# Attention woven into a feed-forward kernel: fewer tile visits, a re-timed plan, and sums moved to GpSimd

## The chip, the cores and the metric

The kernel runs on one core of a Trainium2 chip. A core has five engines that run side by side, each through its own instructions in order: TensorE (PE in the profile; its weight loads are PEld), VectorE (DVE), ScalarE (ACT), GpSimd (POOL), and SyncE (SP), which here issues the DMAs. They wait for each other by semaphores. The metric is the device time of one execution, in microseconds; lower is better.

## The reference

A macaron block on `x` of 8 x 512 x 512 numbers in float32: half a feed-forward block, attention, and half a feed-forward block again, each behind a layernorm.

```python
x = x + 0.5 * ffn(layernorm(x));  x = x + attn(layernorm(x));  x = x + 0.5 * ffn(layernorm(x))

# ffn: 512 -> 2048 -> 512
h = silu(x @ w_gate) * (x @ w_up)
h = keep, in each group of four neighbours, the two of largest magnitude
return h @ w_down

# attn: 16 query heads of 32, 4 key/value heads (tiled over the query heads), rotary positions
scores = einsum('bhqd,bhkd->bhqk', Qr, Kr) / HEAD_DIM ** 0.5
out = einsum('bhqk,bhkd->bhqd', softmax(scores), V_rep)
return out.reshape(b, s, d) @ W_o
```

## The kernel before

There are 8 batches and two feed-forward blocks for each, so 16 blocks (`blocks`). Attention of one batch runs beside the feed-forward products of another, and so does the layernorm of the next block. All instructions are written in one order by a Python program that plans as it goes: `at` holds a clock for TensorE, VectorE and ScalarE, `takes` books a step on one of them with a time written in the code, and `later`/`soon` put VectorE work into queues that `fill` empties when it fits beside TensorE's clock. `ensure` runs the queued work that a step depends on at once. Nothing is moved afterwards: each engine gets its instructions in the order in which the program names them.

*Feed-forward.* Gate and up are computed by a scheme with seven products of half-size blocks (`woven`, L604) in place of eight; their sums of weight quarters (S1 to S4) are made once, in the first block, by VectorE (`combine_gu`, L673), and stored to DRAM. One such product is four matmuls of 128 x 128 by 256 in the program, eight in the trace, as each float32 matmul runs as two. The down product does the same (`products`, L532), with five sums of down-weight quarters (`SUMS`) for each half of the hidden size, also made in the first block: `combine_down` loads 1 MB (`raw`), VectorE adds (L482), SP stores (L483). After each chunk of 512 hidden numbers, `keep_two_of_four` makes the selection on VectorE (L392 to L418) in two halves, and GpSimd makes the sums of `h` that the down products take (L424 to L429).

*Attention.* For each batch: layernorm, projections with rotary positions, then four groups `c` of four query heads. TensorE works these in tiles of 32 rows (`sc`, the scores, L817; `st`, the transposed scores, L850 and L855) or 32 columns (`ops`, the weighted values, L865; `den`, the denominators, L883), four heads side by side. For each of four blocks of keys `t`, ScalarE makes `p = exp(st)` (L858) and VectorE adds up the `p` of the blocks in place (`summed`, L157 in the profile since queued work is run from one line); `den` then takes the sum of the last one, and `divided` (L880 on) divides by a logarithm and an exponential. Scores of group `c + 1` are computed ahead, VectorE finds their maxima (`nm`), `in_pieces` splits these into three bfloat16 parts (`z`), and `pieces_by_row` transposes them (`tr`), for a subtraction inside the next `st`. `sc` and `st` share one PSUM buffer, `p` has two buffers, and all other products share three PSUM banks (`Bank`), taken in rotation.

*The visits.* `attention` is a generator. At each `yield` it hands back a function that tells when it may go on; the main loop at the end runs feed-forward products, counts them in `n` (0.5 for a product of `woven`, 1 for a down product), and goes on with a side stage when `n` is past its `due` and its inputs are ready by the plan. So a visit is a stretch of attention's matmuls between feed-forward products. Before the change, each block `t` of keys has two visits, one with `weighted(t - 1)` and `scores(c + 1, t)`, one with `exponentials(c, t)`, and each group has one more, with `weighted(NT - 1)` alone. `WEIGHTS` gives the share of time for each visit.

Of the kernel before, what the change touches and what calls it, by code (L numbers as in the profile page):

```python
# [18 lines left out]
P = 128  # L19
# [7 lines left out]
def macaron_block(  # L27
# [123 lines left out]
    class Later:  # L151
# [8 lines left out]
        def fits(self, slack):  # L160
            return max(at["dve"], self.ready) + self.us <= at["pe"] + slack

# [76 lines left out]
    def transposed(parts):  # L239
# [5 lines left out]
        takes("pe", 0.65 if kind == FP else 0.45)  # L245
# [5 lines left out]
    def now():  # L251
        return 0.0

    in_xT = []

    def layernorm_t(got, tag, src=None, xb=None):
# [54 lines left out]
        if xb is None:  # L311
# [11 lines left out]
            yield now  # L323
            for t in range(NT):
                normalise(t)
                end = at["act"]
                yield now if t < NT - 1 else lambda: end if len(in_xT) < 2 else None
            for t in range(NT):
                turn(t)
                yield now  # L330
# [40 lines left out]
    def keep_two_of_four(h, made, sums=None, halves=(0, 1)):  # L371
# [14 lines left out]
        for half in halves:  # L386
# [32 lines left out]
            if sums is not None:  # L419
# [5 lines left out]
                else:  # L425
# [3 lines left out]
                    nc.gpsimd.tensor_tensor(h21, h21, h11, ALU.subtract)  # L429
            thin["halves"] = half + 1  # L430
# [15 lines left out]

    gu_made, written = {}, {}
# [21 lines left out]
    def combine_down():  # L469

        for c in range(NCH):
# [8 lines left out]
            def combine(i, name, c=c, quarter=quarter, sums=sums):  # L480
                op = ALU.add if name[2] == "+" else ALU.subtract
                nc.vector.tensor_tensor(sums[:, i], quarter[name[:2]], quarter[name[3:]], op)  # L482
# [20 lines left out]
    def ffn(b, final, last):  # L503
# [9 lines left out]
        def products(hs, g):  # L513

            operands = []

# [4 lines left out]
            def product(i):  # L521
# [17 lines left out]
                takes("pe", 3.69)  # L539
# [17 lines left out]
        def down(h, w, c, t):  # L557
# [7 lines left out]
            takes("pe", 3.62)  # L565
# [6 lines left out]
        def hidden(h, i, r, cols):  # L572

            n = cols.stop - cols.start
            for m in range(2):
# [6 lines left out]
                takes("pe", 3.62 * n / S)  # L582
# [10 lines left out]
        def woven(h, i, r, last_one):  # L593
# [5 lines left out]
            def product(bank, q, rhs, first, ready=0.0):  # L599
# [12 lines left out]
                takes("pe", 1.83)  # L612
# [139 lines left out]
    def attention(b):  # L752
# [15 lines left out]
        def projected(dst, col, scale):  # L768
# [6 lines left out]
            takes("pe", 3.62)  # L775
# [28 lines left out]
        takes("pe", 3.75)  # L804
# [8 lines left out]
        def scores(c, t, nm):  # L813
# [6 lines left out]
            takes("pe", 1.15)  # L820
# [24 lines left out]
        def exponentials(c, t, mT):  # L845
# [10 lines left out]
            takes("pe", 1.45)  # L856
# [5 lines left out]
        def weighted(t, ops, p):  # L862
# [5 lines left out]
            takes("pe", 1.1)  # L868

        def summed(p, before):  # L870
# [219 lines left out]
```

## Time and profile before

| what | value |
|---|---|
| time, median of 3 runs | 3265.1 us (3264.68 to 3265.1) |
| profiled execution: time, span | 3262.97 us, 3261.2 us |
| granted TensorE clock over the span | 0.997 |
| busy in the first 125 us: TensorE, VectorE, GpSimd | 101.21, 85.32, 15.66 us |
| busy from 125 us on: TensorE, VectorE, GpSimd | 3098.76, 2176.40, 548.61 us |
| sums of exponentials on VectorE | 384, 248.4 us, 700 ns each |
| down sums on VectorE | 20, 14.3 us, 757 ns each |
| ScalarE's table loads | 216, 277.1 us |

The span runs from the first to the last instruction of the core. Busy time of TensorE is drawn from modelled ends and overlapping rows; the start times of its matmuls are the firmer reading. In a row of the waits, the engine, line and tile that waited stand first, then whom it waited for, then the total in us, how often, and the longest. In the timeline, the first number is the start in us, the second the duration; brackets at the end hold the idle time just before and who ended it.

### The profile page before, as it was taken

The page shows a single profiled execution, that of the slowest core. Times are in us where ns is not written, and L with a number is a line of the kernel's source. Part 1 is how long each engine was busy: PE and PEld are TensorE (multiplying, and loading weights), DVE is VectorE, ACT ScalarE, POOL GpSimd, SP SyncE. Part 2 cuts the span into 40 slices and gives each one's busy share as a digit, 9 for nine tenths or more (in the row PEclk, how much of TensorE's full clock was granted, in tenths as well). Part 3 has the DMA queues.
Part 4 walks back from the last instruction along what each step waited for, and adds up shares of the span by engine and source line. Part 5 has one row for each costly group of instructions (what it writes and reads, how often), then busy time and mean ns, then how long its engine had stood idle before and what let it go on. Part 6 is the DMA issues. An engine that isn't in the chain of part 4 may idle for free.

```text
span 3261.2 us, 43693 instructions
## 1 busy us (share of the span) xinstructions
PE 3200.0 (98%) x15880; PEld 2316.7 (71%) x15880; DVE 2261.7 (69%) x4892; ACT 1196.7 (37%) x1686; POOL 564.3 (17%) x868
## 2 busy tenths in 40 slices
PE   7999999999999999999999999999999999999999
PEld 5786667766667677766776668766766678666886
DVE  6767775778577775776578865777577765777554
ACT  2222552155324451354314442155325542255221
POOL 0221112210130112110221111211120121201120
PEclk9999999999999999999999999999999999999999
DMA  7563334543433444334453345433533436234451
GB/s 244 196 221 108 116 127 145 174 130 101 158 134 126 136 139 162 133 118 138 143 172 129 110 154 176 140 119 117 196 97 115 155 126 210 91 117 135 156 174 46
DMA packets 249285, 463.21 MB, mean 142 GB/s; under 512 B 24432, under 2 KB 64368, under 8 KB 248304
## 3 DMA queue, kind: packets, MB, share of 16 engines
q1 hardware_dynamic: 249072, 460.42, 42.9%
q8 instruction: 127, 2.08, 0.3%
q14 instruction: 86, 0.70, 0.1%
HBM read 421.53 MB, written 38.80 MB: 141 GB/s over the span
## 4 chain that ended last, share of the span: by engine, by line
PE 92%; DVE 4%; DMA 2%; ACT 1%; issue 0%; POOL 0%; SPq 0%; DVEq 0%; ACTq 0%
PE x L604 25%; PE y L532 23%; PE v L604 12%; PE z L604 6%; PE proj L772 4%; PE sc L817 4%; PE st L850 4%; PE ops L865 4%; PE y L944 3%; PE tr L244 1%; PE gu L579 1%; DMA xn<-x 1%; DVE nm L157 1%; PE den L883 1%; PE vps L797 1%; PE y L562 1%
## 5 line engine op out<-in xcount | busy, mean ns | idle before, releaser
L604 PE MATMUL x<-ts,w 128*128 128x256 f32 x3000 | 721.5, 383 | 10.7 <-DVE corner L618 9.2
L604 PEld LDWEIGHTS x<-ts,w 128*128 128x128 f32 x3000 | 560.0, 190 | 165.5 <-issue 50.1
L532 PE MATMUL y<-wd,h 128*128 128x256 f32 x1984 | 457.3, 385 | 12.0 <-DVE h L418 6.3
L532 PEld LDWEIGHTS y<-wd,h 128*128 128x128 f32 x1984 | 375.8, 192 | 101.3 <-issue 32.0
L858 ACT ACTIVATE p<-st 128x2048 f32<-128x2048 f32 x128 | 239.6, 1872 | 400.7 <-PE st L855 233.2
L424 POOL TENSOR_TENSOR e<-h 128x512 f32<-128x512 f32 x62 | 89.3, 1440 | 1615.4 <-DVE h L418 1442.7
L157 DVE TENSOR_REDUCE nm<-sc 128x1 f32<-128x512 f32 x512 | 320.2, 681 | 68.8 <-PE sc L817 66.9
L532 PE MATMUL y<-wd,e 128*128 128x256 f32 x1488 | 337.3, 381 | 0.2 <-PE den L883 0.2
L545 DVE SCALAR_TENSOR_TENSOR x<-y,x 128x512 f32<-128x512 f32 x372 | 241.9, 683 | 130.2 <-PE y L532 128.6
L532 PEld LDWEIGHTS y<-wd,e 128*128 128x128 f32 x1488 | 279.7, 190 | 62.3 <-issue 18.7
L236 ACT ACT_TABLE_LOAD x216 | 277.1, 1283 | 4.5 <-PEq L1079 0.7
L224 ACT COPY row<-x 128x512 f32<-128x512 f32 x212 | 124.1, 585 | 392.5 <-PE x L604 392.1
L157 DVE TENSOR_TENSOR p<-p 128x512 f32<-128x512 f32 x384 | 248.4, 700 | 10.4 <-PE ops L865 10.4
L653 ACT ACTIVATE h<-x 128x256 f32<-128x256 f32 x125 | 47.5, 380 | 558.1 <-PE x L604 525.0
L604 PE MATMUL v<-xT,w 128*128 128x256 f32 x1000 | 241.5, 385 | 5.7 <-DVE corner L226 5.7
L604 PE MATMUL v<-ts,w 128*128 128x256 f32 x1000 | 240.1, 383 | 1.1 <-DVE h L157 1.1
L604 PE MATMUL x<-xT,w 128*128 128x256 f32 x1000 | 240.5, 383 | 0.0
L604 PE MATMUL z<-xT,w 128*128 128x256 f32 x1000 | 240.0, 383 | 0.0
L604 PEld LDWEIGHTS v<-xT,w 128*128 128x128 f32 x1000 | 187.3, 191 | 57.3 <-issue 13.2
L604 PEld LDWEIGHTS x<-xT,w 128*128 128x128 f32 x1000 | 185.3, 190 | 57.4 <-issue 30.6
L604 PEld LDWEIGHTS v<-ts,w 128*128 128x128 f32 x1000 | 186.8, 190 | 54.8 <-issue 20.8
L604 PEld LDWEIGHTS z<-xT,w 128*128 128x128 f32 x1000 | 185.8, 190 | 52.6 <-issue 22.9
(106 smaller groups left out, 4010.4 us busy)
## 6 DMA issues: line engine op xcount, KB each, us to landing
w<-gu SPq DMA_DIRECT2D x472, 256.0 KB, 3.3
w<-in_w_gu SPq DMA_DIRECT2D x394, 256.0 KB, 3.3
wd<-wd SPq DMA_DIRECT2D x155, 512.0 KB, 3.8
wd<-in_w_down SPq DMA_DIRECT2D x124, 256.0 KB, 5.0
x<-x SPq DMA_DIRECT2D x64, 256.0 KB, 2.6
xn<-x SPq DMA_DIRECT2D x64, 256.0 KB, 7.0
x<-in_x SPq DMA_DIRECT2D x32, 256.0 KB, 3.4
gu<-w SPq DMA_DIRECT2D x32, 256.0 KB, 2.6
```

The source lines that it names most:

```text
L157: self.does()
L224: nc.scalar.copy(dst, src)
L236: nc.scalar.activation(dummy[:, 1:2], dummy[:, 0:1], f)
L532: nc.tensor.matmul(out=y.tile[:, t, :], lhsT=part[:, t * P : (t + 1) * P], rhs=operands[i][:, n, :], start=(n == 0), stop=(n == 3),)
L545: nc.vector.scalar_tensor_tensor(to, y.tile, 0.5 * sign, to, ALU.mult, ALU.add)
L604: nc.tensor.matmul(out=bank.tile[:, m, :], lhsT=lhs[:, m, k, :], rhs=rhs[:, k, :], start=(first and m == 0 and k == 0), stop=(k == 1), ski ...
L772: nc.tensor.matmul(out=ps.tile, lhsT=wa[:, k, col : col + P], rhs=xT[:, k, :], start=(k == 0), stop=(k == ND - 1))
L817: nc.tensor.matmul(out=sc[:, kv, :], lhsT=qT[rows, c, t * P : (t + 1) * P], rhs=kT[rows, :], start=True, stop=True)
L850: nc.tensor.matmul(out=st[:, kv, :], lhsT=kT[rows, t * P : (t + 1) * P], rhs=qT[rows, c, :], start=True, stop=False)
L858: nc.scalar.activation(p, st, AF.Exp)
L865: nc.tensor.matmul(out=ops[rows, :], lhsT=v[:, t, rows], rhs=p[:, kv, :], start=(t == 0), stop=(t == NT - 1))
L944: nc.tensor.matmul(out=y.tile, lhsT=qT[:, k, t * P : (t + 1) * P], rhs=wo[:, k, :D], start=(k == 0), stop=(k == ND - 1))
```

## The change

Five things change together.

- **The plan's times.** `multiplied` books TensorE's steps with new, shorter times and adds `SWITCH` where the shape changes between whole and tiled matmuls. `Bank` takes the bank that comes free first instead of the next in rotation. A fourth clock stands for GpSimd.
- **Visits.** `weighted(NT - 1)` moves into the next group's first visit, `divided` and `in_pieces` move behind `exponentials` into its visit, and in the last group, where there are no scores, the two visits of a block of keys become one.
- **Sums of exponentials.** Of the four heads, GpSimd sums two and VectorE two.
- **Down sums.** GpSimd makes all of them, issued at once and not queued, in two stages at other places (from `n` = 11 and from 22, not from 9 to 25).
- **Layernorm.** Normalising and transposing wait until ScalarE's booked time is at most `BEHIND` = 2 us ahead of TensorE's (`by_scalar`).

```diff
-    HEARD, TOLD = 0.2, 0.15
-    at = {"pe": 0.0, "dve": 0.0, "act": 0.0}
+    HEARD, TOLD, SWITCH, BEHIND = 0.2, 0.15, 0.1, 2.0
+    at = {"pe": 0.0, "dve": 0.0, "act": 0.0, "pool": 0.0}
...
+    tiled = [False]
+
+    def multiplied(us, tiles=False):
+
+        takes("pe", us + (SWITCH if tiles != tiled[0] else 0.0))
+        tiled[0] = tiles
...
+    class Done:
+
+
+        def __init__(self, end):
+            self.end = end
...
     class Bank:
         def __init__(self, shape, name, dtype=FP):
-            self.slot = banks.popleft()
+            self.slot = min(banks, key=lambda slot: max(slot[2], when(slot[1]), at["pe"]))
+            banks.remove(self.slot)
...
+    def by_scalar():
+
+        return at["act"] - BEHIND
...
-            yield now
+            yield by_scalar
             for t in range(NT):
                 normalise(t)
                 end = at["act"]
-                yield now if t < NT - 1 else lambda: end if len(in_xT) < 2 else None
+                yield by_scalar if t < NT - 1 else lambda: max(end, by_scalar()) if len(in_xT) < 2 else None
...
-    def combine_down():
-
-        for c in range(NCH):
+    def combine_down(g):
+
+        for c in range(2 * g, 2 * g + 2):
             raw = p_slots.tile([P, 4, D], FP, "raw")
             nc.sync.dma_start(out=raw, in_=w_down[c])
...
-            def combine(i, name, c=c, quarter=quarter, sums=sums):
+            for i, name in enumerate(SUMS):
                 op = ALU.add if name[2] == "+" else ALU.subtract
-                nc.vector.tensor_tensor(sums[:, i], quarter[name[:2]], quarter[name[3:]], op)
-                nc.sync.dma_start(out=combined[c // 2, name][:, c % 2 * 2 : c % 2 * 2 + 2, :], in_=sums[:, i])
-
-            for i, name in enumerate(SUMS):
-                made = later(0.7, partial(combine, i, name), at["pe"], for_later)
-            p_slots.used(wa_slots.used(made))
+                nc.gpsimd.tensor_tensor(sums[:, i], quarter[name[:2]], quarter[name[3:]], op)
+                nc.sync.dma_start(out=combined[g, name][:, c % 2 * 2 : c % 2 * 2 + 2, :], in_=sums[:, i])
             yield now
-        ensure([made])
+        done_down.add(g)
...
-                takes("pe", 1.83)
+                multiplied(1.73)
...
-            takes("pe", 1.15)
+            multiplied(1.07, True)
...
         def summed(p, before):
 
             if before is None:
                 return []
-            for kv in range(N_KV):
-                made = later(0.6, partial(nc.vector.tensor_tensor, p[:, kv], p[:, kv], before[:, kv], ALU.add))
-            return [p_slots.used(p_slots.used(made), 1)]
+            for kv in (2, 3):
+                nc.gpsimd.tensor_tensor(p[:, kv], p[:, kv], before[:, kv], ALU.add)
+            made = [Done(takes("pool", 2.6, pe_heard()))]
+            for kv in (0, 1):
+                made.append(later(0.6, partial(nc.vector.tensor_tensor, p[:, kv], p[:, kv], before[:, kv], ALU.add)))
+            for one in made:
+                p_slots.used(p_slots.used(one), 1)
+            return made
...
-        last, end = None, 0.0
+        p = before = last = None
+        out_of = []
         for c in range(ND):
             ensure(pieces)
             mT = pieces_by_row()
             turned = at["act"]
             nm = maxima()
-            p = before = None
-            found, sums = [], []
             for t in range(NT):
-                if t:
-                    if t == 1:
-                        ops = acc_slots.tile([P, S], FP, "ops")
-                    weighted(t - 1, ops, p)
+
+
+                if t == 1:
+                    ops = acc_slots.tile([P, S], FP, "ops")
+                if p is not None:
+                    weighted((t - 1) % NT, ops, p)
                 if c + 1 < ND:
                     found = scores(c + 1, t, nm)
-                if t:
+                if p is not None:
                     sums = summed(p, before)
-                elif last is not None:
-                    out_of = divided(*last)
-                yield partial(lambda f, turned: max(when(f), turned), found, turned)
-                before = p
+                    before = p if t else None
+                    if t == 0:
+                        last = (c - 1, ops, p, sums)
+                if c + 1 < ND:
+                    yield partial(lambda f, turned: max(when(f), turned), found, turned)
                 p, end = exponentials(c, t, mT)
-                yield partial(lambda end: end, end)
-            weighted(NT - 1, ops, p)
-            if c + 1 < ND:
-                pieces = in_pieces(nm)
-            last = (c, ops, p, summed(p, before))
-            yield partial(when, pieces + last[3])
+                there = []
+                if t == 0 and last is not None:
+                    there = out_of = divided(*last)
+                elif t == NT - 1 and c + 1 < ND:
+                    there = pieces = in_pieces(nm)
+                yield partial(lambda there, end: max(when(there), end), there, end)
+        weighted(NT - 1, ops, p)
+        last = (c, ops, p, summed(p, before))
+        yield partial(when, last[3])
...
-    WEIGHTS = [0.5] * (NORM + ND + 2) + [0.7] * (NT + 1) + [0.9] * (ND * (2 * NT + 1) + 1) + [0.5] * NT
-    ATTENTION = NORM + ND + 2 + NT + 1 + ND * (2 * NT + 1) + 1 + NT
+    WEIGHTS = [0.5] * (NORM + ND + 2) + [0.7] * (NT + 1) + [0.9, 0.9] * NT
+    WEIGHTS += ([0.9, 1.5] + [0.9, 0.9] * (NT - 1)) * (ND - 2) + [1.5] + [1.3] * (NT - 1) + [0.9] * 2 + [0.5] * NT
+    ATTENTION = len(WEIGHTS)
...
-    sides = [(9, 25, 3 * NCH, combine_down, None, None)]
+    sides = [(11, 18, 6, partial(combine_down, 0), None, None), (22, 32, 6, partial(combine_down, 1), None, None)]
```

The other times of `takes("pe", ...)` are replaced in the same way: 3.69 by 3.46 and 3.62 by 3.43 for whole products, 1.45 by 1.29 (`st`), 1.1 by 1.0 (`ops`), 1.6 by 1.0 (`den`), 0.65 by 0.44 and 0.45 by 0.32 (transposes).

More of the change, by code (lines that the diff above doesn't have):

```diff
@@ L244, in transposed @@
             nc.tensor.transpose(tr.tile[:, c, :], part, ident if kind == FP else identb)
-        takes("pe", 0.65 if kind == FP else 0.45)
+        multiplied(0.44 if kind == FP else 0.32)
         return tr
@@ L429, in keep_two_of_four @@
                     nc.gpsimd.tensor_tensor(h21, h21, h11, ALU.subtract)
+                takes("pool", 1.3 if half == 0 else 5.2, at["dve"] + 0.5)
             thin["halves"] = half + 1
@@ L445, in begin @@
         thin["next"] = next(steps)
+    done_down = set()
     gu_made, written = {}, {}
@@ L538, in product @@
                         )
-                takes("pe", 3.69)
+                multiplied(3.46)
                 load()
@@ L564, in down @@
                 )
-            takes("pe", 3.62)
+            multiplied(3.43)
             fill()
@@ L581, in hidden @@
                     )
-                takes("pe", 3.62 * n / S)
+                multiplied(3.43 * n / S)
                 fill()
@@ L774, in projected @@
                 )
-            takes("pe", 3.62)
+            multiplied(3.43)
             fill()
@@ L803, in attention @@
                 )
-        takes("pe", 3.75)
+        multiplied(3.57)
         fill()
@@ L855, in exponentials @@
                 nc.tensor.matmul(out=st[:, kv, :], lhsT=ones[rows, :], rhs=mT[rows, :], start=False, stop=True)
-            takes("pe", 1.45)
+            multiplied(1.29, True)
             function(AF.Exp)
@@ L867, in weighted @@
                 )
-            takes("pe", 1.1)
+            multiplied(1.0, True)
         def summed(p, before):
@@ L883, in divided @@
                 nc.tensor.matmul(out=den.tile[rows, :], lhsT=ones32, rhs=p[:, kv, :], start=True, stop=True)
-            takes("pe", 1.6)
+            multiplied(1.0, True)
             rT = w_slots.tile([P, S], FP, "rT")
@@ L946, in attention @@
                 )
-            takes("pe", 3.65)
+            multiplied(3.43)
             fill()
```

3 lines of the change are left out of this document (2 added, 1 removed).

## The prediction

> **What bounds the kernel now.** I read the busy line and the chain first, to learn which engine sets the end; then the waits of that engine; then the timeline of the opening and of one attention stretch; then groups of rows for prices.
>
> ```profile
> PE 3200.0 (98%) x15880; PEld 2316.7 (71%) x15880; DVE 2261.7 (69%) x4892; ACT 1196.7 (37%) x1686; POOL 564.3 (17%) x868
> PE 92%; DVE 4%; DMA 2%; ACT 1%; issue 0%; POOL 0%; SPq 0%; DVEq 0%; ACTq 0%
> ```
>
> TensorE is busy 98% and holds 92% of the chain. The change takes no matmul away, so it can only gain at places where TensorE waits, or in what a matmul costs by its neighbours. The waits of TensorE, the largest rows:
>
> ```profile
> PE x L604 <- DVE corner L618: 9.2, 4, 3.7
> PE tr L244 <- DVE xn L345: 7.4, 3, 6.3
> PE sc L817 <- DVE nm L157: 6.9, 7, 1.4
> PE y L532 <- DVE h L418: 6.3, 2, 3.3
> PE v L604 <- DVE corner L226: 5.7, 1, 5.7
> PE y L532 <- DVE row L618: 5.7, 2, 3.0
> PE st L850 <- DVE nm L157: 4.8, 5, 1.4
> PE den L883 <- DVE row L618: 3.1, 5, 0.6
> PE den L883 <- DVE x L545: 2.8, 2, 1.6
> ```
>
> All rows of that view add to 57 us, nearly all on VectorE. I sort them by place: the opening (first 125 us) 23 us, of which 7.4 are the start itself; attention's scores, exponentials and denominators 6.9 + 4.8 + 7.2 = 19 us; the side work around layernorms (two waits for `row`, 5.7; the other `corner` waits, 5.5; and some small ones) 13 us. In the opening the granted clock is also 0.93, against 1.00 after it, since waits near 3 us or longer are followed by a stretch at half clock: the 12 matmuls at 101.34 below took 4.78 us, while 16 take 3.45 elsewhere. That adds some 7 us there.
>
> ```profile
> 50.88 2.02 DVE L673 TENSOR_TENSOR w<-w 128x512 f32<-128x512 f32 x3 [5.41 <-DMA w<-in_w_gu]
> 54.75 3.44 PE L604 MATMUL x<-ts,w 128*128 128x256 f32 x8 [3.74 <-DVE corner L618]
> ...
> 77.71 1.42 DVE L157 TENSOR_TENSOR h<-h,row 128x512 f32<-128x512 f32 x1
> 78.54 1.71 POOL L427 TENSOR_TENSOR e<-h 128x512 f32<-128x512 f32 x1
> ...
> 96.46 3.08 DVE L482 TENSOR_TENSOR sums<-raw 128x512 f32<-128x512 f32 x5
> 101.34 4.78 PE L532 MATMUL y<-wd,h 128*128 128x256 f32 x12 [3.33 <-DVE h L418]
> ```
>
> VectorE stands in order behind a late DMA (50.88), and then TensorE stands behind VectorE (54.75). Five down sums (L482) lie just ahead of the work that the product at 101.34 needs. The middle pair is a collision: both operands of `h<-h,row` are in SBUF, and beside GpSimd it took 1.42 us instead of its usual 0.68; GpSimd took 1.71 instead of 1.27.
>
> ```profile
> 1011.48 1.89 PE L604 MATMUL v<-ts,w 128*128 128x256 f32 x8
> 1013.20 1.89 PE L604 MATMUL x<-ts,w 128*128 128x256 f32 x8
> 1015.02 1.14 PE L850 MATMUL st<-qT,kT 32*128 32x512 f32 x8
> 1015.99 0.40 PE L855 MATMUL st<-mT,ones 3*128 3x512 bf16 x4
> ```
>
> By start times a product takes 1.72 us before another product and 1.82 before tiled work. So a change of tile shape costs 0.09 us. (Starts count: the shown durations overlap.)
>
> **The change, part by part.**
>
> *Fewer visits.* By the built instruction order, runs of tiled matmuls fall from 328 to 272, and changes of tile shape from 744 to 688, as merged visits still change between shapes inside. 56 x 0.093 = **-5.2 us**, all on TensorE's path. Leaving a shape for another is seen only for `ops` to `sc` (1.00 us for the `ops` step, the same as before a product), so I take the new pair `ops` to `st` at that.
>
> *Spacing of visits.* With the old plan a product is booked at 1.83 us and takes 1.73 (about 1.755 with a short break of 0.10 us every 28 to 32 matmuls, which stays as the instruction count does). The old plan so believes that inputs are ready about 4% too early. Counting products between visits, 40 of the 328 begin under 3.4 us after the one before, in the new order 4, all between the first scores. Four maxima need 2.48 us plus 0.14 after the scores, so such a gap waits. Of the 11.7 us in scores and exponentials I keep 4/7 of the 6.9, the share of the close score pairs (7 before, 4 now): **-7.8 us**, ends 0 and -11.7.
>
> *Denominators.* `divided` moves from the head of a group's first visit to behind its `st`, and the banks are chosen by when they come free. The 7.2 us of waits before `den` were mostly for banks: I take 5 of them as gone (ends 0 and 7.2). But in each batch's last head group no scores lie between: the order there is `tr`, `ops`, `st`, `den` in one visit. The sums that `den` reads can begin only when `ops` has read `p` (they write in place), and two of them are now GpSimd's. From the end of `ops`, GpSimd needs 0.2 + 2 x 1.27 = 2.75 us (the L426 to L429 rows lie at 1.26 to 1.28 undisturbed), or 0.2 + 2 x 1.72 = 3.64 if VectorE's own two sums collide with it, as they start at the same moment; `st` covers 1.29 (1002.64 to 1003.93 in another stretch). So TensorE waits 1.46 to 2.35, and the planner does not see it: `ensure(sums)` has no effect on its TensorE clock. I take 1.9, since the two engines start together, for 8 batches: **+15 us**, ends 11.7 and 18.8. Behind `den`, the next products wait. Net of the bank waits: **+10**.
>
> *Sums of exponentials.* VectorE loses 192 of 384, at 0.70: -134 us of its time. GpSimd gains 192 at 1.27 to 1.44: 245 to 276 us, so 564 becomes some 820 with the next part, 25% of the span, no bound by amount. It works beside the four maxima after the scores, which read PSUM: those kept 0.68 beside GpSimd's long rows in this trace. Price of the lock elsewhere: over the 367 long GpSimd rows the excess of VectorE's rows above their medians is 60 us, 0.16 us each; 212 more give +34 us. Then ScalarE's `exp`, which waits for a `p` buffer, waits on two engines: `p<-st` stands 160 us behind VectorE's sums today, mean 5.2. In the last head group `exp` begins some 1.3 to 2.1 us later than `st` would allow; five of its gaps have only 3.55 us, up to 1 us each. Collisions and these gaps together: **+3 us**, ends -5 (a lighter VectorE is early elsewhere) and +15 (each of the 96 pairs of sums makes its visit late by the 0.16 us of a mean collision).
>
> On the same place the Trainium skill, "SBUF — State Buffer", section "SBUF: two separate sides", goes further: the port pair is an exclusive lock, held for the whole instruction, and the loser fully blocks. If each of the 212 moved sums blocked one VectorE row for 1.27 us, VectorE would gain 269 - 149 = 120 us of work instead of losing some 100, and the second rival would be the forecast. The rows speak for much less, as rows that read PSUM are not blocked here.
>
> *Down sums by GpSimd.* VectorE loses 20 x 0.757 = 15 us in a 125-us stretch where it is busy 85 and late. GpSimd is idle until 70 us, so the first five cost nothing; the second five stand behind the first `e`, which waits for VectorE's `h`. Their stores and the loads of gate and up weights behind them share SP's queue: 5 x 1.27 = 6.4 us of waiting there. I count from the order that these loads are needed one group of seven products (12 us) later, which covers it; if VectorE is late by more, this comes back. The raw load that now stands ahead of the 50.88 loads moves one group on, ahead of loads with 2 to 3 us more room. Gains: 4.5 of the 54.75 wait with its slow clock, 3 to 5 at 101.34, 2.5 of 5.7 at 81.19, nothing sure at 118.57: **-12 us**, ends -20 and +3.
>
> *Layernorm steps by ScalarE's clock.* Normalising waits until ScalarE's booked time is within 2 us of TensorE's. This can help the two 3-us waits near 917 and 2373, but their first cause, GpSimd's chain of small steps (ACT `xn` waited 51 us for it in all), is not in the plan, and now has sums ahead of it: **-3 us** of 13, ends -8 and +4. The order also gives VectorE 20 copies more at 0.69, 14 us, beside products.
>
> *Sum.* -5.2 - 7.8 + 10 + 3 - 12 - 3 = **-15 us**. The profiled execution has a span of 3261.2 and a time of 3262.97; the median is 2.1 above that. So span 3246, median 3265.1 - 15 = **3250 us**.
>
> **Rivals.**
> 1. *GpSimd's share is hidden*: the denominators find their sums made because TensorE is late there anyway, and the lighter VectorE removes more waits. For it: 57 us stand on VectorE. Against it: the dependence is direct, with 1.29 us of cover. -5.2 - 11.7 - 5 (banks) - 16 (opening, between my value and its end) - 3 = -41: 3224.
> 2. *Slower, by the port lock*: GpSimd's sums block VectorE's two-input rows, so VectorE is later, not earlier. For it: 0.68 became 1.42 at 77.71, and a cast of 0.20 took 1.21 at 1451. Against it: the maxima are immune and fill most of the sum's time. The point of turning is 135 us of saved VectorE time (149 less the 14 of copies) at 0.74 a collision: 182 collisions among 212 sums. Then opening, layernorm and spacing gain 0, and the denominators and sums are at their ends: -5.2 + 13.8 + 15 = +24: 3289.
> 3. *The pieces cancel*: the denominators' wait is at its upper end, and the opening gives half: -5.2 - 7.8 + 13.8 + 3 - 6 + 0 = -2: 3263. The plan then only changes places of waits.
>
> **How the numbers follow.** A measurement here tells about 0.2% (6.5 us). Forecast, -7 to -35: 0.50. Rival 1: 0.12. Rival 3, within 6.5 us either way: 0.15. Rival 2 and other losses: 0.23. So faster 0.62, same 0.15, slower 0.23. The range leaves a tenth beyond each end: 3220, just past rival 1's time, and 3284, short of rival 2's by the smaller half of its chance. The forecast's own range is 3230 to 3258.
>
> **What would show it.** Right: waits of `sc` and `st` on `nm` at some 4 us together; a new row, `den` waiting on GpSimd, eight times near 1.9; no L482 on VectorE and the wait at 54.75 gone; GpSimd near 820 busy; TensorE's busy time some 5 us less. Wrong: `den` waits above 3 us each, VectorE busy above 2200 (lock), new waits for `w` DMAs in the first 125 us, or no `den` row at all.

## The result, and the profile after

The changed kernel takes 3277.16 us (median of 6 runs, 3272.83 to 3277.46) against 3264.8 us for the kernel before on the same chip (3262.74 to 3265.1). The ratio is **1.0036**, with an interval of 1.0026 to 1.0047: slower by some 12 us, where 15 us less were forecast. The profiled execution spans 3275.3 us, at a granted clock of 0.997 as before.

The busy line and the chain of the kernel after:

```profile
PE 3210.9 (98%) x15880; PEld 2323.2 (71%) x15880; DVE 2264.8 (69%) x4700; ACT 1185.7 (36%) x1670; POOL 879.1 (27%) x1080
```

```profile
PE 88%; DVE 8%; POOL 2%; issue 1%; DMA 1%; ACT 0%; SPq 0%; DVEq 0%; POOLq 0%; ACTq 0%
```

VectorE executes 192 rows fewer and is busy for 2264.8 us, 3 us *more* than before. Its share of the chain has doubled, from 4% to 8%. GpSimd gained 212 rows and 315 us.

TensorE's start times separate work from waiting. I took for each kind of matmul the usual time to the next start, with 0.093 us for a change of shape, and called what is above it waiting. So counted, TensorE's work fell from 3147.1 to 3141.9 us, and its waits grew from 105.0 to 128.3 us. (Some 30 us of these waits are short breaks of 0.10 us, which every version has.) This count is a little high: after a wait inside a group of tiled matmuls a later gap comes out shorter than usual, and that is not taken off. From TensorE's first start to its last there are 3250.6 us before and 3264.8 after, so the waits net of such gaps are 103.5 and 122.9 us, 19.4 more; in the table further down they are 1.5 to 7.5 us too high in the same way. Three parts of the growth can be placed, 19.0 us together: waits in the first 200 us fell by 11.5 (30.5 to 19.05), those inside or ahead of `den` rose by 18.7 (8.0 to 26.7), and those ahead of `sc`, `st` and the transposes of `z` rose by 11.8 (13.4 to 25.2). The largest rows of TensorE's waits, after:

```profile
PE st L867 <- DVE nm L164: 13.0, 12, 1.7
PE x L621 <- DVE corner L635: 7.6, 3, 5.8
PE tr L258 <- DVE xn L363: 7.3, 3, 6.2
PE tr L258 <- DVE z L850: 5.7, 4, 1.8
PE den L905 <- DVE p L164: 4.9, 12, 2.3
PE sc L834 <- DVE nm L164: 4.1, 4, 1.4
```

`sc` on `nm` fell from 6.9 to 4.1, but `st` on `nm` rose from 4.8 to 13.0, and `den` on `p` is new. The `den` row names VectorE's half of the sums only. One visit in the last head group shows what is in it. The timeline from 444.93 us, first TensorE, then VectorE, then GpSimd:

```profile
444.93 1.06 PE L882 MATMUL ops<-p,v 128*32 128x512 f32 x8
445.92 1.14 PE L867 MATMUL st<-qT,kT 32*128 32x512 f32 x8
446.88 0.40 PE L872 MATMUL st<-mT,ones 3*128 3x512 bf16 x4
447.21 1.04 PE L905 MATMUL den<-p,ones 128*32 128x512 f32 x2
448.43 2.17 PE L905 MATMUL den<-p,ones 128*32 128x512 f32 x6 [0.17 <-DVE p L164]
450.53 1.78 PE L621 MATMUL z<-xT,w 128*128 128x256 f32 x7
...
446.01 2.36 DVE L164 TENSOR_TENSOR p<-p 128x512 f32<-128x512 f32 x2 [0.51 <-PE ops L882]
...
446.20 3.30 POOL L892 TENSOR_TENSOR p<-p 128x512 f32<-128x512 f32 x2 [7.99 <-PE ops L882]
```

Both engines begin when `ops` has ended and run side by side. VectorE's two sums took 2.36 us, where two of 0.68 would take 1.36; GpSimd's two took 3.30, where its undisturbed rows of this size lie at 1.27 each. From the first `den` at 447.21 to the next product at 450.53 there are 3.32 us for eight small matmuls. By start times this stretch waits 2.33 us; the eight such visits wait 2.32, 2.33, 2.40, 2.32, 2.40, 2.33, 3.25 and 2.33 us, 19.7 together.

The sums on both engines, as groups (busy us, then mean ns of one):

```profile
L892 POOL TENSOR_TENSOR p<-p 128x512 f32<-128x512 f32 x192 | 276.0, 1457 | 779.0 <-PE ops L882 585.5 <-issue 52.9 <-ACT row L238 49.4
L164 DVE TENSOR_TENSOR p<-p 128x512 f32<-128x512 f32 x192 | 169.1, 915 | 27.8 <-PE ops L882 27.5 <-POOL e L445 0.3
```

A sum on VectorE took 700 ns before and 915 now. The collision is not confined to the sums themselves. The timeline at 2933 us, first VectorE, then GpSimd, then TensorE:

```profile
2933.22 0.28 DVE L419 TENSOR_TENSOR m<-m 128x256 bf16<-128x256 bf16 x1
2933.41 1.35 DVE L420 TENSOR_TENSOR m<-m 128x256 bf16<-128x256 bf16 x1
2934.69 1.35 DVE L422 TENSOR_TENSOR m<-m 128x256 bf16<-128x256 bf16 x1
2935.97 0.28 DVE L423 TENSOR_TENSOR m<-m 128x256 bf16<-128x256 bf16 x1
2936.57 2.47 DVE L164 TENSOR_REDUCE nm<-sc 128x1 f32<-128x512 f32 x4
...
2933.35 2.54 POOL L892 TENSOR_TENSOR p<-p 128x512 f32<-128x512 f32 x2 [8.02 <-PE ops L882]
...
2933.12 1.14 PE L834 MATMUL sc<-kT,qT 32*128 32x512 f32 x8
2939.10 1.14 PE L867 MATMUL st<-qT,kT 32*128 32x512 f32 x8 [1.19 <-DVE nm L164]
```

The `scores` end near 2934.3, but the four maxima stand behind the selection's bfloat16 steps in VectorE's order. Each of GpSimd's two sums (1.27 us) holds one of those steps for 1.35 us in place of 0.28. That makes the maxima 2.1 us later, and `st`, which needs the PSUM buffer that they read, waits 1.19 us. This is one of the twelve waits in the new 13.0 us row. In nine others too, VectorE's rows ahead of the maxima are longer than usual, by 1.1 to 3.3 us together; the last two (at 781.0 and 2246.8) show nothing of it and are there without GpSimd's sums as well.

ScalarE is held up too: its `exp` waits 77.1 us for GpSimd's sums, in 13 places. But TensorE's waits have no row of `ops` waiting for `p`, so this lateness did not reach it.

Over the whole trace I added, for each VectorE row that overlapped a GpSimd row longer than 0.6 us, its time above the median of its kind. Before, this gives 59.7 us beside 367 such rows; after, 171.9 us beside 582. The 215 added rows cost VectorE 112 us, **0.52 us each**. With the sums back on VectorE 61.4 us of this excess are left, so nearly all of the growth is theirs.

### The profile page after: what moved, and what is told of

Read it like the earlier page. It is cut to its first block, busy times and chain, and to the rows that moved or that the text cites. A ratio compares the mean times of both kernels' runs of the same rounds, so it can differ in the third digit from the quotient of the medians.

```text
span 3275.3 us, 43750 instructions
## 1 busy us (share of the span) xinstructions
PE 3210.9 (98%) x15880; PEld 2323.2 (71%) x15880; DVE 2264.8 (69%) x4700; ACT 1185.7 (36%) x1670; POOL 879.1 (27%) x1080
## 4 chain that ended last, share of the span: by engine, by line
PE 88%; DVE 8%; POOL 2%; issue 1%; DMA 1%; ACT 0%; SPq 0%; DVEq 0%; POOLq 0%; ACTq 0%
PE x L621 24%; PE y L549 22%; PE v L621 12%; PE z L621 6%; PE proj L789 4%; PE sc L834 4%; PE y L971 3%; PE ops L882 3%; PE st L867 3%; DVE nm L164 2%; PE tr L258 1%; PE gu L596 1%; PE den L905 1%; POOL p L892 1%; PE vps L814 1%
## 5 line engine op out<-in xcount | busy, mean ns | idle before, releaser
L892 POOL TENSOR_TENSOR p<-p 128x512 f32<-128x512 f32 x192 | 276.0, 1457 | 779.0 <-PE ops L882 585.5
L238 ACT COPY row<-x 128x512 f32<-128x512 f32 x196 | 114.7, 585 | 411.6 <-PE x L621 410.9
```

Of the source, the lines that this page charges most:

```text
L238: nc.scalar.copy(dst, src)
L892: nc.gpsimd.tensor_tensor(p[:, kv], p[:, kv], before[:, kv], ALU.add)
```

## The experiments

Three theories stood against each other. The first: the moved sums block VectorE's rows (the port lock of the prediction), and this takes back what VectorE was to be spared. The second: the loss lies in the order alone, since in the last head group `den` stands in the visit whose `ops` its sums wait for. The third: the new times of the plan cost or bring something by themselves. Every ratio below is to the kernel before, run in turn on the same chip. A difference between two ratios is uncertain by about 0.2%, if their intervals are combined by squares.

| kernel | ratio (interval) | TensorE's waits, us | VectorE above its medians beside long GpSimd rows, us |
|---|---|---|---|
| before | 1 | 105.0 | 59.7 |
| after | 1.0036 (1.0026 to 1.0047) | 128.3 | 171.9 |
| after, sums on VectorE | 0.9983 (0.9974 to 0.9992) | 106.7 | 61.4 |
| after, `den` in its own visit | 0.9992 (0.9982 to 1.0001) | 110.3 | 166.8 |
| after, sums on VectorE, idle sums on GpSimd | 1.0082 (1.0067 to 1.0097) | 139.5 | 138.3 |
| before, two heads' sums on GpSimd | 1.0232 (1.0215 to 1.0249) | 186.4 | 199.8 |
| after, both repairs | 0.9948 (0.9933 to 0.9963) | 92.4 | 58.5 |
| the same, visits wait for their sums | 0.9959 (0.9944 to 0.9974) | 97.5 | |
| before, down sums on GpSimd | 0.9951 (0.9935 to 0.9968) | 91.3 | |
| before, new plan | 1.0007 (0.9998 to 1.0016) | 108.0 | |
| before, down sums, new visits, `den` apart | 0.9941 (0.9926 to 0.9956) | 92.2 | |
| before, down sums, bank that is free first | 0.9953 (0.9937 to 0.9970) | | |
| both repairs, two heads' sums left out | 0.9874 (0.9856 to 0.9892) | 72.5 | 67.7 |

**The sums of all four heads back on VectorE.** The rest of the change stays.

```diff
-            for kv in (2, 3):
-                nc.gpsimd.tensor_tensor(p[:, kv], p[:, kv], before[:, kv], ALU.add)
-            made = [Done(takes("pool", 2.6, pe_heard()))]
-            for kv in (0, 1):
-                made.append(later(0.6, partial(nc.vector.tensor_tensor, p[:, kv], p[:, kv], before[:, kv], ALU.add)))
-            for one in made:
-                p_slots.used(p_slots.used(one), 1)
-            return made
+            for kv in range(N_KV):
+                made = later(0.6, partial(nc.vector.tensor_tensor, p[:, kv], p[:, kv], before[:, kv], ALU.add))
+            return [p_slots.used(p_slots.used(made), 1)]
```

> The changed kernel, with the sums of exponentials of all four heads on VectorE again; everything else of the change stays. Theory A (the port): GpSimd's sums hold up VectorE's rows that have two operands in SBUF, so VectorE got no time back (its busy time was 2261.7 before and 2264.8 after), and TensorE waits for late maxima. Then the excess of VectorE's rows over their medians falls from 172 to about 60 us, the waits at st, sc and tr fall from 25 to about 13 us, the wait at den in the last head group goes from 2.3 to about 1.4 us (four sums at 0.6 on one engine against 1.29 us of cover), and the time is about 3277 - 12 - 7 = 3258. Theory B (the dependence alone): only den gets better, by 7 us: about 3270, and st keeps its waits. The forecast's own view (the sums help): slower than 3277.

Measured: 0.9983. The change is faster than before without its last part, by 0.53% (17 us) against the change as it is. The busy line, and the two rows of TensorE's waits on `nm`:

```profile
PE 3208.1 (99%) x15880; PEld 2324.0 (71%) x15880; DVE 2274.2 (70%) x4894; ACT 1194.6 (37%) x1680; POOL 603.1 (19%) x888
```

```profile
PE sc L834 <- DVE nm L164: 4.1, 4, 1.4
PE st L867 <- DVE nm L164: 1.6, 3, 0.8
```

VectorE makes 192 sums more and is busy only 9 us longer than after. `st` on `nm` is 1.6 us, not 13.0, with the same visits. But the last head group still waits at `den`: 14.8 us over its eight visits, 1.85 each and not the 1.4 expected. So the second theory is not dead either.

**`den` in a visit of its own in the last head group.** GpSimd keeps its two heads.

```diff
                 if t == 0 and last is not None:
+                    if c + 1 == ND:
+                        yield partial(lambda sums, end: max(when(sums), end), last[3], end)
                     there = out_of = divided(*last)
```

The share of time of the first visit, 1.5, is split into two of 0.75.

> The changed kernel, with one more visit in each batch's last head group: den waits for the plan's end of the sums in a visit of its own, not behind st. GpSimd still sums two heads. Theory B (the dependence alone costs the loss): the 19.7 us of waits at these eight den visits go, less 8 x 2 x 0.093 = 1.5 us of shape changes: about 3259. Theory A (the port): these waits go as well, but st, sc and tr keep their 25 us, so 3259 to 3262 by this term, and a kernel with all sums on VectorE and the same extra visit would be another 12 us faster. Both theories are told apart by the st and sc waits, which stay by A.

Measured: 0.9992, or 0.44% (14 us) less than after. The eight waits of 2.46 us are gone; the `den` of the last group waits 11.6 us in all of its 16 places, from 22.8. What stays:

```profile
PE st L867 <- DVE nm L164: 12.9, 12, 1.6
PE den L905 <- POOL p L892: 3.3, 4, 1.5
```

The waits of `st` are as they were, and so is VectorE's excess, 166.8 us. The two losses are separate: one goes with the place of `den`, the other with GpSimd's sums.

**As many rows on GpSimd, with no later step in need of their result.** VectorE makes all sums as in the first experiment, and GpSimd adds an idle tile to itself, twice for each pair of blocks. A one-column row that reads `p` holds it back until `exp` has made `p`; the moved sums begin later, when `ops` has read it.

```diff
+    gate = const.tile([P, 1], FP, name="gate")
+    idle = const.tile([P, S], FP, name="idle")
...
+            nc.gpsimd.tensor_tensor(gate, p[:, 2, 0:1], p[:, 3, 0:1], ALU.add)
+            for kv in (0, 1):
+                nc.gpsimd.tensor_tensor(idle, idle, idle, ALU.add)
```

> The kernel of the first run of this set (all sums on VectorE), and GpSimd does as many sums of the same size on a scratch tile that nobody reads, each pair begun when the exponential is there. Same port use, no dependence. Theory A: VectorE's excess goes back up by 60 to 110 us, st and sc waits come back, and the time is 10 to 20 us over that of the first run. Theory B: within 3 us of the first run.

Measured: 1.0082, which is 0.99% (32 us) above the first experiment, where 10 to 20 were expected. The groups of sums, on VectorE and idle on GpSimd:

```profile
L167 DVE TENSOR_TENSOR p<-p 128x512 f32<-128x512 f32 x384 | 276.6, 774 | 31.4 <-PE ops L885 28.7 <-POOL gate L894 2.6
L896 POOL TENSOR_TENSOR idle<-idle 128x512 f32<-128x512 f32 x192 | 212.7, 1108 | 7.5
```

No engine needs the idle sums, and VectorE waits only 2.6 us for the row that holds them back. Still VectorE's busy time goes from 2274.2 to 2346.3 us, and TensorE's waits from 106.7 to 139.5. So rows on GpSimd cost the kernel time by running, whatever their result is for. That is the mechanism of the first theory, though it reaches TensorE by another way here. The waits for late maxima did not come back as expected: `st` on `nm` is 3.4 us (1.6 in the first experiment, 13.0 after). In their place VectorE's own sums are longer (774 ns, 723 in the first experiment), `exp` waits for them 245.3 us in place of 199.5, and `ops` waits for `exp`, 10.4 us in place of 3.1:

```profile
PE ops L885 <- ACT p L878: 10.4, 9, 4.2
```

**The kernel before, with only two heads' sums moved.**

```diff
-            for kv in range(N_KV):
+            for kv in (2, 3):
+                nc.gpsimd.tensor_tensor(p[:, kv], p[:, kv], before[:, kv], ALU.add)
+            for kv in (0, 1):
```

> The kernel before, with the sums of exponentials of two of four heads given to GpSimd and nothing else (old plan, old visits, down sums on VectorE; the plan books nothing for GpSimd). There den stands behind a visit of its own, so the dependence has cover. Theory A: slower than before by 8 to 20 us with VectorE's busy time not lower than 2240. Theory B: within 5 us of before, or faster by the relief.

Measured: 1.0232, 76 us slower, far beyond the 8 to 20 expected. Two rows of TensorE's waits:

```profile
PE st L850 <- DVE nm L157: 23.4, 19, 3.3
PE den L885 <- POOL p L875: 8.0, 6, 2.5
```

The same sums cost far more here than in the changed kernel. Here the plan does not know how long GpSimd takes, visits stand closer, and the last denominators wait up to 7.63 us. So something in the new visits and the new plan with its fourth clock hid much of the damage; which of them was not tested. The granted clock fell to 0.990.

**Both repairs together**: the sums on VectorE and `den` apart, by the two diffs above.

> The changed kernel with both repairs: all sums of exponentials on VectorE, and den in the last head group in a visit of its own, after the sums by the plan. Theory A and B together (the port and the dependence each cost what the first two runs of the earlier set showed): the 14.8 us of den waits in the last group that were left with all sums on VectorE go, less 1.5 us of shape changes: about 13 us below the 3256.6 of that kernel, 3243, which is 19 under the kernel before. If the two overlap instead (each repair hides the same waits): 3254 to 3257.

Measured: 0.9948. The gains add up: 0.35% from the first experiment (by the visit), 0.44% from the second (by the sums). This is 17 us less than before.

**The same, where a visit of `st` and `den` is held until its sums should be made.**

```diff
-                    yield partial(lambda f, turned: max(when(f), turned), found, turned)
+                    waits = found + sums if t == 0 and c else found
+                    yield partial(lambda f, turned: max(when(f), turned), waits, turned)
```

> The kernel of both repairs, and in the other head groups too the visit with st and den waits, by the plan, for the sums that den reads (no further visit, only a later one). With all sums on VectorE 10 us of waits at den stood in these 16 visits, as four sums are behind the four maxima there. If they can be taken away by waiting in the plan: 5 to 10 us below the run with both repairs. If the waits only move to the products that follow: the same within 3 us.

Measured: 0.9959, not told apart from the version without it. The waits of `den` behind `st` fell from 10.1 to 4.5 us, but one row of TensorE's waits grew from 2.8 to this:

```profile
PE ops L882 <- DVE qT L164: 10.2, 6, 2.3
```

All waits together are 97.5 against 92.4 us: the waits moved, as the second expectation said.

**The down sums alone, in the kernel before.** The edit is `combine_down(g)` and the two stages in `sides`, as the change has them, and nothing else of it.

> The kernel before, with the down sums given to GpSimd at their new places and nothing else. The changed kernel lost 11.5 us less than the kernel before in its first 200 us. If that comes from the down sums alone: 11 us faster than before, and the waits after 200 us are unchanged. If it came from the plan's new times: within 4 us of before.

Measured: 0.9951, 16 us less than before. TensorE's waits fall from 105.0 to 91.3, and of these 13.7 us, 13.4 lie in the first 200 us. This part carries nearly the whole gain that the change holds. Engine and places changed together here, so how much is due to each is not shown.

**The plan alone, in the kernel before**: the new times, `SWITCH`, the choice of banks and `by_scalar`, with the old visits and sums.

```diff
-                takes("pe", 1.83)
+                multiplied(1.73)
...
-            self.slot = banks.popleft()
+            self.slot = min(banks, key=lambda slot: max(slot[2], when(slot[1]), at["pe"]))
```

> The kernel before, with the new plan alone: the shorter times, the bank that comes free first, layernorm by ScalarE's clock. Visits, sums and down sums as before. My own step said that the old plan's long times made visits follow each other too closely and cost 7.8 us at sc and st, and 3 at layernorms: then about 10 us faster than before, with sc and st waits near 4 us. If the closeness was harmless or the cause another: within 4 us of before. The rest of the way to the kernel with all sums on VectorE is then for the visits (5.2 us of shape changes) and the down sums.

Measured: 1.0007, no difference. TensorE's waits on `nm`:

```profile
PE sc L837 <- DVE nm L164: 7.6, 8, 1.4
PE st L870 <- DVE nm L164: 4.9, 6, 1.4
```

They are as before. Of its visits, 38 still begin under 3.4 us after the one before (40 in the kernel before, 4 after). So the third theory falls: the new plan alone neither spaces the visits nor saves anything in sum.

**The visits with the old plan**: the down sums on GpSimd, the change's loop over visits and its shares of time, `den` apart; old times, banks in rotation, sums on VectorE.

> The kernel before with the down sums on GpSimd, the new visits and den apart in the last group, all sums of exponentials on VectorE; the old plan (its times, banks in rotation, no ScalarE clock at layernorms). It is the run with both repairs without the new plan. The order has only 4 visits closer than 3.4 us, where the new plan with the old visits still had 38: so by the order the visits, not the times, take the closeness away. If the visits do what they promise (5.2 - 0.7 us of shape changes, sc and st waits down by up to 8, less new den waits of up to 10): 3 to 8 us under the kernel with down sums alone, so a ratio near 0.993, and the same as or better than the run with both repairs. If the visits need the new plan: slower than the run with both repairs by 5 or more.

Measured: 0.9941, the lowest of the kernels that compute the reference, but not told apart from the run with both repairs (0.9948) or from the down sums alone (0.9951). Here 4 visits are close, and `sc` on `nm` is this:

```profile
PE sc L814 <- DVE nm L157: 4.1, 4, 1.4
```

So it was the merging of visits, not the plan's times, that removed the close ones. Beside the down sums alone the visits are worth 0.1%, which these runs do not tell from nothing.

**The choice of banks, with the down sums.** The down sums alone, and the `min(banks, ...)` shown above.

> The kernel before with the down sums on GpSimd and the bank that comes free first; nothing else. The waits before den for banks (some 5 of 7.9 us) go if the choice of banks does it: 3245, 3 us under the kernel with down sums alone. If those waits are for the sums: no change.

Measured: 0.9953, as without it (0.9951). The waits ahead of `den` hardly moved; this row, for one, is as long as in the kernel before:

```profile
PE den L881 <- DVE row L616: 3.1, 5, 0.6
```

So the choice of the bank does not take them away.

**Two heads' sums left out.** As both repairs, but only heads 0 and 1 are summed (by VectorE), and `den` takes these for heads 2 and 3 as well. So this kernel does not compute the reference; it shows what VectorE's relief would be worth if GpSimd's work cost nothing.

```diff
-            for kv in range(N_KV):
+            for kv in (0, 1):
...
-                nc.tensor.matmul(out=den.tile[rows, :], lhsT=ones32, rhs=p[:, kv, :], start=True, stop=True)
+                nc.tensor.matmul(out=den.tile[rows, :], lhsT=ones32, rhs=p[:, kv % 2, :], start=True, stop=True)
```

> The kernel with both repairs, with the sums of exponentials of heads 2 and 3 left out altogether: nobody makes them, and their denominators are taken from the sums of heads 0 and 1, so these parts of the output are not the reference's. It shows what 134 us less of VectorE time is worth without GpSimd in the way. The kernel with den apart and GpSimd's sums stood at 0.9992 of before, the one with all sums on VectorE at 0.9948. If relief is worth nothing, as TensorE hardly waits for VectorE there: 0.994 to 0.995, and the whole 0.0044 (14 us) is the price of the port and of waiting for GpSimd. If relief is worth something: 0.990 or less, and the price of GpSimd's sums is that much higher, 25 us or more.

Measured: 0.9874. The busy line:

```profile
PE 3188.6 (99%) x15880; PEld 2318.1 (72%) x15880; DVE 2156.3 (67%) x4683; ACT 1195.2 (37%) x1685; POOL 603.2 (19%) x888
```

VectorE is relieved by 115 us against both repairs (2271.6), and the kernel gains 0.74%, 24 us. With GpSimd making those sums (the second experiment, the same in all else) the time is 1.18% or 38 us higher, and TensorE's waits are 110.3 against 72.5 us, which is the same 38 (36 net of shortened gaps). So moving the sums pays 24 us and costs 38: 14 us lost, as the second experiment and both repairs show directly (0.9992 against 0.9948). The 24 us hold whatever a lighter VectorE brings, `den` finding its sums sooner too; the 38 us hold all that GpSimd's work brings, the rows that it lengthens and the waits for its results. These are not split further.

## Why the prediction was wrong

The forecast was 15 us less, and it became 12 us more. By the runs, the 12 us split as follows, with 3265 us for a ratio of 1: the down sums -16; plan, visits and layernorm, with `den` apart, -1 (0.9951 to 0.9948, not told from 0); `den` in the visit of its own sums +11 (0.9948 to 0.9983); two heads' sums to GpSimd +17 (0.9983 to 1.0036). The sum is +11. Each difference is uncertain by some 5 to 8 us. Two steps failed: the sums of exponentials, +17 (+14 with `den` apart) where +3 stood, and the small gains of visits, spacing and layernorm, -1 where -16 stood. The down sums, -16 for -12, made up a little of it.

*What bounds the kernel*: right. TensorE sets the end, its work changes only by shape, and everything else is waiting.

*Fewer visits, -5.2*: right. TensorE's work without waits fell by 5.2 us, as the count of 56 shape changes at 0.093 gave it. (The sign "TensorE's busy time some 5 us less" did not come: the busy line, drawn from modelled ends, shows 10.9 us more.)

*Spacing of visits, -7.8*: half right, and put to the wrong cause. With the sums on VectorE the waits on `nm` fell from 11.7 to 5.7 us. I had tied this to the old plan's long times; the plan alone kept the close visits, the visits with the old plan lost them. And the text took for granted that maxima come 2.48 us plus 0.14 after the scores. That holds only if VectorE starts them at once. With GpSimd's sums it was held in the rows ahead of them, and the same waits were 17.1 us, not the "some 4 us" named as the sign.

*The small gains together*: **they failed too.** -5.2, -7.8 and -3 make -16; with `den` apart and the sums on VectorE, -1 was measured, and even the end of its interval is -8. The waits named in the prediction did shrink: `nm` by 6.0 us, `y` on `row` from 5.7 to 0.4. But the text counted them as saved, and the new order and plan made others. Three rows of TensorE's waits in the run with both repairs that the run with the down sums alone does not have:

```profile
PE tr L258 <- DVE z L850: 3.6, 2, 1.8
PE v L621 <- ACT rT L904: 3.2, 1, 3.2
PE ops L882 <- DVE qT L164: 2.8, 2, 1.4
```

Together with the waits of `den` behind `st`, 10.1 us, these use up what was saved: all waits of the two runs are 92.4 and 91.3 us. How much each of the three would bring alone stays open.

*Denominators*: the mechanism was right, and it showed eight times as said. The size was off: 2.46 us each in place of 1.9, 19.7 in all, just over the upper end of 18.8. Seven of the eight lie between 2.32 and 2.40, so the upper of my two values for one wait, 2.35, the one with collisions, was the usual one and not an end: both pairs wait for the same `ops` and must start together. Most of the wait comes from the order, though, and not from GpSimd: with all sums on VectorE 14.8 of the 19.7 us stay. GpSimd's pair took 3.30 us in the visit shown, near two of 1.72. The 5 us of bank waits were not to be had, as the run with the new choice of banks shows.

*Sums of exponentials, +3*: **the step that turned a gain into a loss.** I took 0.16 us for a long GpSimd row, the mean over all of them in the old trace, wherever they stood, and so +34 us on VectorE; how these become +3 on the kernel, the text does not work out. The added rows cost 0.52 us each, 112 us on VectorE in all, and 14 to 17 us of the kernel's time. Their place differs: they start when `ops` ends, and at that moment VectorE starts its own two sums, or is in the selection's steps, whose operands are in SBUF. The maxima, which are indeed not slowed, come only after these. VectorE's time by count should have gone down by 135 us (149 less 14 of copies), but the durations of its rows add up to only 13.2 us less (2555.2 to 2542.0). Only 24 us of TensorE's time hung on this relief at all, so it could not have paid for much. The sign "VectorE busy above 2200" was the right one, and it came: 2264.8.

*The rule weighed there.* The Trainium skill, "SBUF — State Buffer", section "SBUF: two separate sides", says that the loser blocks for the whole instruction. A single collision in this trace is that: 0.28 us became 1.35 beside a row of 1.27. My objection, that rows reading PSUM escape, was true as well, and the mean lies between: 0.52 us, as if one in two of the added rows had cost what that collision did, 1.07. Between the 0.16 that I took and the 1.27 of the rule I should have counted which VectorE rows run when the sums start, and not averaged over all places.

*Down sums, -12*: right in sum, by other parts than named. The waits of the first 200 us fell by 11.5 after, and the part alone gave 16 us. The busy time by stage (TensorE, its weight loads, VectorE, ScalarE, GpSimd) shows GpSimd at 47 us, from 16, in the opening:

```profile
0.00:125.00 125.00, 108.63 (x439) 85.45 (x440) 91.57 (x186) 28.39 (x52) 47.24 (x49) 0.97 0.72 248
```

The wait at 101.34 shrank to 0.17 us, as argued. The one at 81.19 (5.74 us, of which 2.5 were counted) is gone, and the one at 118.57, of which nothing was counted, shrank from 2.95 to 1.55. But the one at 54.75, of which 4.5 us were counted, did not go; it moved behind the next product group and is longer, with the stretch at half speed after it (3.78 us for eight matmuls, 1.89 before it). VectorE's three sums of gate and up weights ahead of it took 4.02 us beside GpSimd's down sums, where 2.02 stood before, which is what it is longer by. That the sum came out near -12 is so in part luck:

```profile
60.87 1.89 PE L621 MATMUL z<-xT,w 128*128 128x256 f32 x8
...
62.23 4.02 DVE L690 TENSOR_TENSOR w<-w 128x512 f32<-128x512 f32 x3 [5.55 <-DMA w<-in_w_gu]
...
68.59 3.78 PE L621 MATMUL x<-ts,w 128*128 128x256 f32 x8 [5.82 <-DVE corner L635]
...
93.80 2.42 PE L549 MATMUL y<-wd,h 128*128 128x256 f32 x10 [0.17 <-DVE h L436]
```

*Layernorm, -3*: not shown. `y` on `row` went from 5.7 to 2.2 us after, but the plan alone, which holds this part, gained nothing in sum, and in the run with the new visits and the old plan, which does not hold it, the row is 0.4 us.

*The rivals.* What came was the second, the port lock, with the denominators at their upper end, as it says. It came out at +12 and not +24, because the lock did not take the opening's gain. The point of turning, 135 us of VectorE's time taken back, was all but reached (122 us). I had given it 0.23 together with other losses; the old trace had a nearer price than the mean that I set against it: 15 of VectorE's sums of exponentials overlapped a long GpSimd row there, and they were 7.2 us longer than usual together, 0.48 us each.

## What to carry to other kernels

Work moved from VectorE to GpSimd is not free for VectorE, even where GpSimd is three quarters idle: look up, in the trace of before, which VectorE rows will run when the moved rows start, and charge each one with its operands in SBUF up to a GpSimd row (here a bfloat16 step lost 1.07 us beside a row of 1.27, and two of VectorE's own sums lost 1.0 together). First ask what the relief is worth by leaving the work out: here 115 us off VectorE was worth only 24 us. And where one visit holds both the step that frees an input and the step that needs what another engine makes of it, split the visit; this one `yield` was worth 11 to 14 us. And a wait that a new order removes is not a gain until all waits are added up again: here 6.0 us on the maxima went and came back elsewhere.

## What the runs showed of the hardware that was not expected

- Small bfloat16 rows are held as well: a `m<-m` row of 128 x 256 went from 0.28 to 1.35 us beside a GpSimd float32 sum, five times its length, while four maxima from PSUM kept their mean of 0.68 us (681 ns before and after).
- GpSimd loses too: its sums took 1457 ns on the mean, with 1.27 us undisturbed, and those of its long rows that took more than 1.27 lay 67 us above it together, against 19 us before. GpSimd's busy time so came to 879.1 us, where some 820 were forecast.
- An idle GpSimd row that reads and writes one tile in place took 1108 ns on the mean, less than a sum of two tiles, and still 192 of them, with 96 rows of one column, cost the kernel 32 us.
- The price of one and the same move depends on the order and the plan around it: two heads' sums on GpSimd cost 76 us in the kernel before and 14 to 17 us in the changed one.
